# First expert tiles loaded in the blocks before, the last two blocks woven in another order, and the last tiles dealt otherwise among the dense experts

## The chip, the cores and the metric

The kernel runs on 1 core of one Trainium2 chip. The metric is device time in microseconds (us) of one execution, and the number compared is the median of several runs. A profile is one execution with the hardware profiler on. Its engines are PE (matrix multiply; PEld is its weight load), DVE (vector), ACT (scalar), POOL (GpSimd) and SP, which here only issues DMAs. "SPq" and "POOLq" in a profile are the queues of SP and POOL.

## The reference, cut to what matters

```python
h = tok_ref(x, W)              # 4 x 4096 tokens of width 256: patches, real FFT, one matmul
x1 = layernorm(h)
n  = layernorm(x1) * g + b
q, k, v = n @ Wq.T + bq, n @ Wk.T + bk, n @ Wv.T + bv
mem[t] = decay * mem[t-1] + k[t] * v[t]          # along 4096 tokens
x1 = x1 + q * mem
x1 = x1 + relu(layernorm(x1) @ W1.T + b1) @ W2.T + b2
h  = h + x1
t  = layernorm(h)
out = h + t
for e in range(8):             # each token uses 2 of 8 experts
    out += combine[:, e:e+1] * (gelu(t @ w1[e] + b1[e]) @ w2[e] + b2[e])
```

## The kernel before, in words

The 16384 tokens are 32 blocks of 512 (`Block`, numbers 0 to 31; `NB` = 32, `NS` = 31). A block goes through three stages, and three blocks are in work at once. In turn `i` of the main loop (L835) the newest block `new` = `i` is embedded (`embed`, L301 and L312), gets its q, k and v and the recurrence (`retention`, L341, matmuls L268), and is added to its residual (`residual`, transposes L391); block `mid` = `i - 1` goes through its MLP (`mlp_in`, L414, matmuls L268; `mlp_out`, L420, matmuls L426) and gives its tokens; block `old` = `i - 2` is routed: `rows` makes rows of 260 words, `logits` and `choose` pick two experts for each token, `place` (L539) finds each row's place and writes the rows to a buffer in device memory, `xbuf`, with eight indirect DMAs on POOL (L560).

Experts work on tiles of 256 rows of `xbuf` that belong to one expert. `take(n, ...)` (L606) makes a table on DVE of the tiles that are full by then and appends them to the list `tiles`: none with block 0's rows, one with block 1's, then four with each block's, and 18 with those of block 30, 131 in all. A tile (`Tile`) has four parts, and each has a counter in `at`:

- `load` (L666): three DMAs on SP. The expert's weights `w` (641.5 KB, L670, 5 buffers), the rows turned by a DMA transpose into `xh` (L677, 6 buffers), four words of each row into `xg` (L680). Addresses come from the table, so SP waits until DVE has written it; the first tile of a `take` also waits until that block's writes to `xbuf` have landed.
- `turn` (L683): ACT puts the halves of `xh` together as `xT` (L687, two copies).
- `enter` (L689): eight matmuls (L694; fp32, so the trace counts two for each) into a `p_mm` buffer, and two Gelu activations on ACT into `ge` (L702).
- `leave` (L706): eight matmuls (L711), then DVE adds the bias and multiplies by the token's share into `y` (L725, L727; 4 buffers), and POOL adds the rows to the output with two indirect DMAs (L731). These two wait until the last two such adds have landed, so tiles add one after the other.

`expert_step` (L807) with `n` tiles entered loads up to tile `n + 3` (`AHEAD` is 4), turns up to tile `n + 1`, enters tile `n` and leaves tile `n - 1`. In the loop it is called by `slot(known)`, four times a turn, once more than three tiles are pending and never so that it would turn a tile of this turn's own `take`. The first step is in turn 5, in its first slot.

SP, PE, DVE and ACT carry out their instructions in the order of the program text (`manual_schedule`); each is a queue in which a waiting instruction holds up all behind it. PSUM pools: `p_mm` has four buffers, for q, k, v, MLP input, `enter` and transposes; `p_tm` has three.

Turning a block from tokens to features is done in two ways. `split1` and `split2` (L330, L403) let ACT split it (L248), a DMA transpose on SP turn it (L256), and ACT or DVE join it (L262). `to_features` (L231) uses eight transposes on PE (L235) and two copies on ACT (L236).

After the loop (L888 to L918) block 31 is `last` and block 30 is `old`. In order: `features2` of 31; two steps; `features3`, `rows`, `logits`, `choose` of 30; a step; `mlp_in` of 31 with `place` and `take` of 30 after its first part (there also eight DMAs on SP that pad the ends of the experts' regions, L584) and a step after its fifth; `mlp_out` of 31 with a step between its halves. Then block 31's own experts: it is not routed through `xbuf`, each of the 8 experts is applied to all its 512 tokens (`Expert`, L743: `enter` 16 matmuls L761, `leave` 16 matmuls L778), and the eight `Expert` items are put into the list with two tiles between each two. Two more steps, `features3`, `logits`, `choose` and `combine` of 31 follow, then steps until the list is empty. The last `Expert` stores block 31 (L795), half on SP, half on ACT's queue.

Tiles are numbered below by their place in the list: 104 to 107 are entered in turn 31, 109 is the first tile with block 29's rows, 113 the first of the 18 with block 30's.

Of the kernel before, what the change touches and what calls it, by code (L numbers as in the profile page):

```python
# [30 lines left out]
def vit_tower_kernel(  # L31
# [20 lines left out]
    E = rw.shape[1]  # L52
    KD, KH = D // P, H // P
    J = STRIDE // 2
    TT = 4
# [10 lines left out]
    NB = B * NBLK  # L66
# [5 lines left out]
    NS = NB - 1  # L72
# [12 lines left out]
    def load_x(i):  # L85
        xb = xpool.tile([P, XW], F32, name="xb")
        nc.sync.dma_start(out=xb, in_=x[i // NBLK, i % NBLK])
        return xb
# [5 lines left out]
    with tc.tile_pool(name="prep", bufs=1) as prep:  # L94
# [8 lines left out]
        xs = {0: load_x(0)}  # L103
# [127 lines left out]
    def to_features(dst, src):  # L231
        for k in range(KD):
            ps = p_mm.tile([P, BLK], F32, name="mm")
            for t in range(TT):
                nc.tensor.transpose(ps[:, ts(t, P)], src[:, t, ts(k, P)], ident)  # L235
            nc.scalar.copy(dst[:, k, :], ps)  # L236
# [40 lines left out]
    class Block:  # L277
# [128 lines left out]

        def features2(self):
            self.hT = two.tile([P, KD, BLK], F32, name="hT")
            if self.i == 0:
                to_features(self.hT, self.zz)  # L410
                return
            self.turn.join(self.hT, nc.scalar.copy)
# [193 lines left out]
    def take(n, block, writes):  # L606

        k = FULL[n] - FULL[n - 1]
        if not k:
            return  # L610
        full = small.tile([1, E], F32, name="full")
        nc.vector.tensor_tensor(full, cnt[0:1, :], first[0:1, :E], ALU.subtract)
        if n == NS:
            nc.vector.tensor_scalar(full, full, float(S - 1), None, ALU.add)
        whole = small.tile([1, E], I32, name="whole")
        nc.vector.tensor_copy(whole, full)
        nc.vector.tensor_scalar(whole, whole, S.bit_length() - 1, None, ALU.arith_shift_right)
        nc.vector.tensor_copy(full, whole)  # L618

        nc.vector.tensor_tensor(full, full, taken, ALU.subtract)  # L620
        upto = small.tile([1, E + 1], F32, name="upto")
        nc.vector.memset(upto[:, 0:1], 0.0)
        nc.vector.tensor_tensor_scan(upto[:, 1:], ones_e, full, 0.0, ALU.mult, ALU.add)

        base = small.tile([1, E + 1], F32, name="base")
        nc.vector.tensor_tensor(base[:, :E], taken, upto[:, :E], ALU.subtract)
        nc.vector.tensor_scalar(base[:, E:], upto[:, E:], -1.0, None, ALU.mult)
        nc.vector.scalar_tensor_tensor(base, base, float(S), first[0:1, :], ALU.mult, ALU.add)
        step = small.tile([1, E], F32, name="step")
        nc.vector.tensor_tensor(step, base[:, 1:], base[:, :E], ALU.subtract)  # L630
        shape = [1, k, E]
        past = small.tile([1, KMAX, E], F32, name="past")[:, :k, :]
        nc.vector.tensor_tensor(
            past,
            tile_f[:, :k].unsqueeze(2).to_broadcast(shape),
            upto[:, 1:].unsqueeze(1).to_broadcast(shape),
            ALU.is_ge,
        )
        table_f = small.tile([1, 2, KMAX], F32, name="table_f")[:, :, :k]
        nc.vector.tensor_reduce(table_f[:, 0, :], past, AX.X, ALU.add)  # L640
        nc.vector.tensor_tensor(past, past, step.unsqueeze(1).to_broadcast(shape), ALU.mult)
        nc.vector.tensor_reduce(table_f[:, 1, :], past, AX.X, ALU.add)
        nc.vector.scalar_tensor_tensor(
            table_f[:, 1, :], tile_f[:, :k], float(S), table_f[:, 1, :], ALU.mult, ALU.add
        )
        table = four.tile([1, 2, KMAX], I32, name="table")[:, :, :k]
        nc.vector.tensor_scalar(table[:, 0, :], table_f[:, 0, :], float(P), float((E - 1) * P), ALU.mult, ALU.min)
        nc.vector.tensor_scalar(table[:, 1, :], table_f[:, 1, :], base[:, 0:1], None, ALU.add)
        if n < NS:
            nc.vector.tensor_scalar(upto, upto, float(k), None, ALU.min)  # L650
            nc.vector.tensor_tensor(taken, taken, upto[:, 1:], ALU.add)
            nc.vector.tensor_tensor(taken, taken, upto[:, :E], ALU.subtract)
        for t in range(k):
            tiles.append(Tile(table, t, block, writes if t == 0 else []))

    AHEAD = 4
    tiles = []
# [142 lines left out]
    at = dict(load=0, turn=0, enter=0, leave=0)  # L800

    def advance(what, upto):
        while at[what] < min(upto, len(tiles)):
            getattr(tiles[at[what]], what)()
            at[what] += 1

    def expert_step():  # L807

        n = at["enter"]
        advance("load", n + AHEAD)  # L810
        advance("turn", n + 2)
        advance("enter", n + 1)
        advance("leave", n)
# [3 lines left out]
    blocks = [Block(i) for i in range(NB)]  # L817
# [3 lines left out]
    def slot(known):  # L821

        if len(tiles) - at["enter"] > LEFT and at["enter"] + 2 <= known:
            expert_step()
# [7 lines left out]
    with tc.manual_schedule(engines=MANUAL):  # L832
        xs[1] = load_x(1)
        blocks[0].differences(xs.pop(0))
        for i in range(NB):  # L835
            new = blocks[i]
            known = len(tiles)
            mid = blocks[i - 1] if i >= 1 else None
            old = blocks[i - 2] if i >= 2 else None
            embed = new.embed()  # L840
            next(embed)
            if mid:
                mid.features2()
            if old:
                old.rows()
                old.turn3()
            next(embed)
            next(embed, None)
            slot(known)
            if old:  # L850
                old.join3()
            if i == 0:
                fold(wqkv_sb, G1, B1, BQ)
            for m in range(KH):
                if mid:
                    mid.mlp_in(m)
                if m == 1 and i:
                    new.split1()
                if m == TT - 1:
                    slot(known)  # L860
                if m == KH - 3:
                    new.features1()
            if old:
                for t in range(TT):
                    old.logits(t)
            if i + 1 < NB:
                blocks[i + 1].differences(xs.pop(i + 1))
            for m in range(KD):
                new.retention(m)
                if old and m == 0:  # L870
                    old.choose()
            if old:
                take(old.i + 1, old, old.place())
            if i + 2 < NB:
                xs[i + 2] = load_x(i + 2)
            slot(known)
            if mid:
                mid.mlp_out(0)
            new.residual()
            slot(known)  # L880
            if i == 0:
                fold(w1_sb.unsqueeze(1), G2, B2, MB1)
            else:
                new.split2()
            if mid:
                mid.mlp_out(1)

        last, old = blocks[NS], blocks[NS - 1]  # L888
        last.features2()
        expert_step()  # L890
        expert_step()
        old.features3()
        old.rows()
        for t in range(TT):
            old.logits(t)
        old.choose()
        expert_step()
        for m in range(KH):
            last.mlp_in(m)
            if m == 0:  # L900
                take(NS, old, old.place())
            if m == TT:
                expert_step()
        last.mlp_out(0)
        expert_step()
        last.mlp_out(1)

        for e in range(E):
            tiles.insert(len(tiles) - 2 * (E - 1 - e), Expert(e, last))
        expert_step()  # L910
        expert_step()
        last.features3()
        for t in range(TT):
            last.logits(t)
        last.choose()
        last.combine()
        while at["leave"] < len(tiles):
            expert_step()  # L918
# [82 lines left out]
```

## Time and profile before

| | |
|---|---|
| runs shown | 2304.29, 2302.86, 2296.04 us (median 2302.86) |
| the profiled execution | 2310.97 us |
| its span, from the first to the last instruction | 2309.2 us |
| PE matmul busy | 2196.0 us (95%) |
| PE weight load busy | 1573.8 us (68%) |
| DVE busy | 1468.9 us (64%) |
| POOL busy | 867.0 us (38%) |
| ACT busy | 790.2 us (34%) |
| DMA engines, busy share | 0.1 to 0.9, by slice |

Some 1.8 us of the execution lie outside its span. The execution that was profiled is 8.1 us above the median of the runs shown. In a group or timeline line the first number is the start (timeline) or the busy time (groups), then come engine, source line, operation, the tile written and the tiles read, sizes and a count; "[15.92 <-ACT xT L687]" behind a timeline line says that the engine had been idle for 15.92 us and that what ended the wait was ACT's instruction that wrote `xT`.

### The profile page before, as it was taken

The numbers are of one execution on the slowest core, as the hardware profiler recorded it, in microseconds if no ns is written. First come the engines' busy times: TensorE is split into PE (matmuls) and PEld (weight loads), VectorE is DVE, ScalarE is ACT, GpSimd is POOL, SyncE is SP. The second block draws the span as 40 slices with busy tenths as digits, with TensorE's granted clock in tenths as the row PEclk, the third lists the DMA queues.
The fourth block names the chain that finished last, engine by engine and source line by source line (L and its number), as shares of the span: only waits on it lengthen the run. The fifth ranks groups of instructions, "written<-read, shape, count | busy, mean of one in ns | idle before, by whom it ended". The sixth has DMA issues, their size and how long they took to land. (4 is left out here: it accounts for less than half of the span.)

```text
span 2309.2 us, 28330 instructions
## 1 busy us (share of the span) xinstructions
PE 2196.0 (95%) x8644; PEld 1573.8 (68%) x8644; DVE 1468.9 (64%) x4358; ACT 790.2 (34%) x1217; POOL 867.0 (38%) x828
## 2 busy tenths in 40 slices
PE   3999979999999999999999999999999999998994
PEld 3576647776676777767667777667677776766773
DVE  6566736666676667666666676666666766665442
ACT  0222233333344333333433333334433333343341
POOL 0012214444433444444344444443344444435334
PEclk8999989999999999999999999999999999999997
DMA  5133365566566765665666656656675566567895
GB/s 148 28 95 76 83 145 124 132 135 143 130 137 137 156 123 133 131 142 129 138 142 156 121 128 139 145 130 134 143 156 122 133 131 141 110 114 181 182 206 89
DMA packets 466920, 304.11 MB, mean 132 GB/s; under 512 B 380369, under 2 KB 434769, under 8 KB 462673
## 3 DMA queue, kind: packets, MB, share of 16 engines
q1 hardware_dynamic: 416864, 234.67, 42.6%
q0 software_dynamic: 49632, 67.39, 16.6%
q8 instruction: 68, 1.11, 0.2%
q14 instruction: 84, 0.68, 0.1%
q10 hardware_dynamic: 272, 0.26, 0.0%
HBM read 131.26 MB, written 88.39 MB: 95 GB/s over the span
## 5 line engine op out<-in xcount | busy, mean ns | idle before, releaser
L731 POOL DMA_INDIRECT out<-y,xg x262 | 435.1, 1661 | 558.0 <-DVE y L727 308.9
L426 PE MATMUL tm<-w_sb,aT 128*128 128x256 f32 x2048 | 462.5, 380 | 11.3 <-issue 7.9
L268 PE MATMUL mm<-hT,w_sb 128*128 128x512 f32 x1024 | 450.9, 593 | 1.7 <-ACT hT L262 1.4
L426 PEld LDWEIGHTS tm<-w_sb,aT 128*128 128x128 f32 x2048 | 386.9, 190 | 76.5 <-issue 23.0
L268 PEld LDWEIGHTS mm<-hT,w_sb 128*128 128x128 f32 x1024 | 194.6, 190 | 222.5 <-issue 211.6
L560 POOL DMA_INDIRECT xbuf<-row,to x248 | 242.7, 979 | 263.0 <-DVE full L618 189.5
L268 PE MATMUL mm<-hT,wqkv_sb 128*128 128x512 f32 x768 | 340.1, 599 | 1.3 <-DVE hT L262 1.2
L702 ACT ACTIVATE ge<-mm,w 128x256 f32<-128x256 f32 x262 | 109.6, 471 | 566.7 <-issue 565.8
L694 PE MATMUL mm<-xT,w 128*128 128x256 f32 x1048 | 256.6, 389 | 27.0 <-ACT xT L687 27.0
L268 PEld LDWEIGHTS mm<-hT,wqkv_sb 128*128 128x128 f32 x768 | 144.5, 191 | 172.2 <-issue 162.7
L418 ACT ACTIVATE aT<-mm,vec 128x512 f32<-128x512 f32 x256 | 172.3, 686 | 242.3 <-PE mm L268 237.5
L711 PE MATMUL tm<-w,ge 128*128 128x256 f32 x1048 | 248.0, 380 | 0.0
L694 PEld LDWEIGHTS mm<-xT,w 128*128 128x128 f32 x1048 | 198.4, 194 | 65.6 <-ACT xT L687 28.2
L312 PE MATMUL tm<-weff,xd 128*128 128x256 f32 x1024 | 229.8, 383 | 11.3 <-DVE xd L289 8.1
L312 PEld LDWEIGHTS tm<-weff,xd 128*128 128x128 f32 x1024 | 195.1, 192 | 42.3 <-DVE xd L289 8.5
L711 PEld LDWEIGHTS tm<-w,ge 128*128 128x128 f32 x1048 | 199.7, 191 | 30.9 <-issue 3.6
L687 ACT COPY xT<-xh 128x512 uint16<-128x512 uint16 x262 | 181.4, 762 | 42.2 <-DMA xh<-xbuf 42.2
L248 ACT COPY planes<-zz 128x1024 uint16<-128x1024 uint16 x124 | 123.5, 1043 | 155.3 <-DVE zz L222 155.1
L213 POOL TENSOR_SCALAR rstd<-mv 128x4 f32<-128x4 f32 x96 | 38.5, 401 | 333.7 <-DVE mv L207 331.5
L725 DVE TENSOR_TENSOR y<-tm,w 128x512 f32<-128x512 f32 x131 | 90.6, 691 | 99.6 <-PE tm L711 63.0
L301 PE MATMUL tm<-wsum,xb 128*128 128x256 f32 x512 | 120.4, 390 | 26.2 <-ACT wsum L118 26.2
L517 POOL TENSOR_TENSOR ex<-euler,second 128x4 f32<-128x4 f32 x32 | 34.5, 1080 | 270.3 <-DVE second L509 270.3
(139 smaller groups left out, 2273.1 us busy)
## 6 DMA issues: line engine op xcount, KB each, us to landing
w<-in_wex SPq DMA_DIRECT2D x139, 641.5 KB
xb<-in_x SPq DMA_DIRECT2D x32, 1040.0 KB
out<-h SPq DMA_DIRECT2D x31, 512.0 KB
out<-y,xg POOLq DMA_INDIRECT x262
xbuf<-row,to POOLq DMA_INDIRECT x248
xh<-xbuf SPq DMA_TRANSPOSE x131
xg<-xbuf SPq DMA_DIRECT2D x131, 4.0 KB
xbuf<-none SPq DMA_DIRECT2D x8, 260.0 KB
```

The costliest lines, as they stand in the source:

```text
L248: nc.scalar.copy(planes[:, :, i * D : (i + 1) * D], half)
L268: nc.tensor.matmul(ps, lhsT=w[:, k, ts(m, P)], rhs=rhs[:, k, :], start=k == 0, stop=k == KD - 1)
L301: nc.tensor.matmul(ps[:, u, :], lhsT=od[:, j, ts(u, P)], rhs=wsum[:, j, :], start=j == 0, stop=j == J - 1)
L312: nc.tensor.matmul(ps[:, i, :], lhsT=xd[:, i, j, ts(u, P)], rhs=weff[:, i * J + j, :], start=j == 0, stop=j == J - 1,)
L418: nc.scalar.activation(self.aT[:, m, :], ps, AF.Relu, bias=vec[:, MB1 + m : MB1 + m + 1])
L426: nc.tensor.matmul(ps[:, i, :], lhsT=self.aT[:, k, ts(u * 2 + i, P)], rhs=w2_sb[:, k, :], start=k == 0, stop=k == KH - 1,)
L560: write = nc.gpsimd.indirect_dma_start(out=xbuf, out_offset=bass.IndirectOffsetOnAxis(ap=to[:, c, t : t + 1], axis=0), in_=self.row[:, t, ...
L687: nc.scalar.copy(halves[:, :, :, 1 - i], self.xh[:, i * KD : (i + 1) * KD, :])
L694: nc.tensor.matmul(ps[:, m, :], lhsT=self.w[:, k * D + m * P : k * D + (m + 1) * P], rhs=self.xT[:, k, :], start=k == 0, stop=k == KD - 1,)
L702: nc.scalar.activation(self.ge[:, m, :], ps[:, m, :], AF.Gelu, bias=self.w[:, 5 * D + m : 5 * D + m + 1])
L711: nc.tensor.matmul(ps[:, c, :], lhsT=self.ge[:, k, ts(c, P)], rhs=w[:, (2 + k) * D : (3 + k) * D], start=k == 0, stop=k == KD - 1,)
L731: add = nc.gpsimd.indirect_dma_start(out=out, out_offset=bass.IndirectOffsetOnAxis(ap=self.xg[:, c, NUMBER - D : NUMBER - D + 1], axis=0), ...
```

## The change

Four edits. (1) In the loop, as long as no tile has been entered, up to two tiles are loaded ahead of `split2`. (2) The loop ends a turn earlier; turn 31 and the code after the loop are written as one piece in another order. Its steps are not held back by `slot`. (3) `features2` of block 31 uses `to_features`. (4) The tiles not yet loaded are dealt evenly ahead of the `Expert` items.

```diff
         def features2(self):
             self.hT = two.tile([P, KD, BLK], F32, name="hT")
-            if self.i == 0:
+            if self.i in (0, NS):
                 to_features(self.hT, self.zz)
                 return
...
-        for i in range(NB):
+        for i in range(NS):
...
             slot(known)
+            if at["enter"] == 0:
+
+                advance("load", 2)
             if i == 0:
                 fold(w1_sb.unsqueeze(1), G2, B2, MB1)
             else:
                 new.split2()
...
-        last, old = blocks[NS], blocks[NS - 1]
-        last.features2()
+        last, mid, old = blocks[NS], blocks[NS - 1], blocks[NS - 2]
+        embed = last.embed()
+        next(embed)
+        mid.features2()
+        old.rows()
+        old.turn3()
+        next(embed)
+        next(embed, None)
+        expert_step()
+        old.join3()
+        for m in range(KH):
+            mid.mlp_in(m)
+            if m == 1:
+                last.split1()
+            if m == TT - 1:
+                expert_step()
+            if m == KH - 3:
+                last.features1()
+        for t in range(TT):
+            old.logits(t)
+        expert_step()
+        mid.mlp_out(0)
+        old.choose()
+        expert_step()
+        mid.mlp_out(1)
+        take(NS - 1, old, old.place())
+        last.retention(0)
+        mid.features3()
+        mid.rows()
+        expert_step()
+        last.retention(1)
+        for t in range(TT):
+            mid.logits(t)
+        mid.choose()
+        last.residual()
         expert_step()
         expert_step()
-        old.features3()
-        old.rows()
-        for t in range(TT):
-            old.logits(t)
-        old.choose()
+        take(NS, mid, mid.place())
         expert_step()
+
+        last.features2()
         for m in range(KH):
             last.mlp_in(m)
-            if m == 0:
-                take(NS, old, old.place())
-            if m == TT:
+            if m in (1, 4):
                 expert_step()
+        expert_step()
         last.mlp_out(0)
         expert_step()
         last.mlp_out(1)

+        rest = tiles[at["load"] :]
+        del tiles[at["load"] :]
         for e in range(E):
-            tiles.insert(len(tiles) - 2 * (E - 1 - e), Expert(e, last))
+            tiles.extend(rest[len(rest) * e // E : len(rest) * (e + 1) // E])
+            tiles.append(Expert(e, last))
```

Counted through, the new piece has twelve steps up to the second half of `mlp_out` of 31 and two behind the dealing; they enter tiles 104 to 117. At the dealing tiles 0 to 118 are loaded, 12 are left, and they go ahead of the experts 0 to 7 as 1, 2, 1, 2, 1, 2, 1, 2. Expert 7 is the last item; tiles 129 and 130 stand ahead of it.

More of the change, by code (lines that the diff above doesn't have):

```diff
@@ L865, in vit_tower_kernel @@
                     old.logits(t)
-            if i + 1 < NB:
-                blocks[i + 1].differences(xs.pop(i + 1))
+            blocks[i + 1].differences(xs.pop(i + 1))
             for m in range(KD):
```

## The prediction

> **What bounds the kernel now.** I read the page first: PE is busy in every slice but a few. The windows then show the end, with the DMA engines' share and GB/s as the last two numbers: full, while PE works.
>
> ```profile
> PE   3999979999999999999999999999999999998994
> ```
>
> ```profile
> 2200.00:2210.00 10.00, 10.00 (x40) 7.30 (x39) 3.05 (x9) 5.59 (x10) 3.86 (x3) 1.00 0.99 222
> ```
>
> So time is won only where PE idles. The waits by length, then the timelines, give the places: one long stop of PE near 300 us, two short ones after 2090 us, and the end.
>
> ```profile
> 294.23 7.07 PE L312 MATMUL tm<-weff,xd 128*128 128x256 f32 x32
> 317.22 3.78 PE L694 MATMUL mm<-xT,w 128*128 128x256 f32 x8 [15.92 <-ACT xT L687]
> ...
> 2100.93 3.47 PE L694 MATMUL mm<-xT,w 128*128 128x256 f32 x8 [6.40 <-ACT xT L687]
> ...
> 2182.36 3.68 PE L694 MATMUL mm<-xT,w 128*128 128x256 f32 x8 [4.71 <-ACT xT L687]
> ...
> 2275.53 3.62 PE L778 MATMUL tm<-w,ret 128*128 128x256 f32 x16
> ```
>
> The reader is to see the three stops, that the eight matmuls behind each take 3.5 to 3.8 us in place of 1.89, and that PE ends at 2279.15, 30 us ahead of the span's end. Those 30 us are POOL's adds (L731), one tile after the other, as the chain of waits shows:
>
> ```profile
> 2281.21 4.25 DMA out<-y,xg
> ...
> 2288.14 3.86 DMA out<-y,xg
> ...
> 2299.28 1.54 POOL out L731
> ```
>
> The first adds of consecutive tiles start at 2174.50, 2184.10, ... 2299.28: 16 intervals, on average 7.8 us; the eight up to 2243.43 average 8.6 (full DMA engines), the last five 6.6.
>
> **First loads.** The first step's loads stand on SP behind four row transposes; ACT idles until they land.
>
> ```profile
> 299.59 2.63 ACT L262 COPY hT<-turned 128x512 uint16<-128x512 uint16 x4 [3.83 <-DMA turned<-planes]
> 302.09 1.98 ACT L453 COPY row<-tok 128x1024 uint16<-128x1024 uint16 x2
> 315.79 1.38 ACT L687 COPY xT<-xh 128x512 uint16<-128x512 uint16 x2 [11.72 <-DMA xh<-xbuf]
> ```
>
> With tile 0 loaded in turn 3 and tile 1 in turn 4, ACT's copy follows its row copies at 304.07 and not at 315.79: 11.7 us, all of it on PE, which had been idle from 301.3; 4.2 us of the stop stay. The three DMAs a tile now stand on SP ahead of `split2`'s transpose, which starts at 241.95 and 295.30. The writes that tile 0 waits for begin on POOL at 227.03, tile 1's at 280.38; the rows below put a tile's `xh` 11.6 us behind that and its three loads' end some 14.5: 241.5 and 294.9, just ahead. Nothing late follows; if each were a landing (4 us) late, `hT` at 299.59 would be too, and the gain 7.7. If the matmuls behind the shorter stop ran at full speed (behind 1.12 us at 283.77 they did), it were 14.3 (1.89 and 0.69 of slow matmuls less). I take 11.7, bounds 7.7 and 14.3.
>
> **Stops removed at the end.** The stop at 2100.93 is `hT` of block 31 (a transposing DMA that ACT awaits) ahead of the tile's copy: eight PE transposes (0.87 us, as the row of L235 between its neighbours) replace it, with two ACT copies of 0.53 for two of 1.0 and four of 0.66 and the transpose on SP. The one at 2182.36 is a late load: its buffer waited for DVE, DVE for `ex` on POOL behind adds. In the new order the same `ex` stands behind two tiles' adds too, but with one tile fewer behind it in DVE; I take both stops out. With the slow matmuls: 6.4 + 1.6 and 4.7 + 1.8.
>
> **Waits added: block 29's rows.** I lay the new order on the old clock, from 2057.23, where `logits` of block 29 end and the two orders part. A step is 3.46 us on PE (1.73 each for `enter` and `leave`), half of `mlp_out` 6.9, `retention` 5.15 a half, `logits` 1.71, transposes 0.87, a part of `mlp_in` 1.72, an expert 6.88. Two steps and both halves of `mlp_out` of 30 end on PE at 2077.95. Then DVE: sum and statistics 2.0, POOL's root 1.5, `tok` 1.4, `h` 1.25: `place` of 29 begins at 2084.2, where before it began at 2070.07, since it now stands behind block 30's tokens on DVE. Behind it go these rows:
>
> ```profile
> 2073.57 1.06 POOL L560 DMA_INDIRECT xbuf<-row,to  x1 [6.53 <-DVE full L618]
> ...
> 2121.67 1.00 POOL L560 DMA_INDIRECT xbuf<-row,to  x1 [0.30 <-issue]
> ```
>
> ```profile
> 2085.15 1.32 SPq L677 DMA_TRANSPOSE xh<-xbuf  x1
> ...
> 2136.10 1.27 SPq L677 DMA_TRANSPOSE xh<-xbuf  x1
> ```
>
> First write 3.5 after `place` begins, `xh` 11.6 after the first write, landing 4.3 (rows: 3.8 to 5.9): 2103.6. On SP the fifth step's three loads (nine DMAs) follow each other; behind them stands nothing that PE needs sooner. The fifth step, between the halves of `retention`, turns tile 109, so ACT waits there; behind it in ACT's queue are `ge` of 108 and `ks` of the second half. Copy 1.4, `ge` 0.7, `ks` 0.7, DVE's recurrence and product 3.1: PE's `residual` can begin at 2109.5. PE has 16.7 us of work from 2077.95 (`place` 0.36, 5.15, 0.87, a step, 5.15, 1.71): 14.9 us idle, the first 6.8 of them because `enter` of 108 needs the `p_mm` buffer of v, which DVE frees only behind `place` and `take`.
>
> **Waits added: block 30's rows.** DVE from 2109.5: `choose` 2.85, residual 3.75, root 1.5, `zz` 1.4, two sums 2.45, then `y` of 108: its adds start on POOL at 2123.2. Those of 109 wait for them (1.9 + 3.75 + 0.85), 2129.7; they take 3.7, and behind them POOL issues block 30's writes, from 2133.4. `xh` of 113 comes 11.6 after that (block 29) to 14.4 (2121.67 to 2136.10, with the padding): I take 13. Landing 4.0, copy and `ge` of 112 2.2: `enter` of 113 at 2152.6 (bounds 2151 to 2156.5). PE arrives there at 2135.2: from 2109.5, 0.87, two steps, 0.36, a step, 0.87, 1.2 for the copies of `hT`, two parts, a step, three parts. 17.4 us idle: the ninth step turns tile 113, 17 us of PE work behind `place`, where before 33 us lay between (2114.56 to 2147.74).
>
> The Trainium skill has a rate for such a load: "DMA: Bandwidth & Descriptors", sections "Latency and other measured facts" and "Anatomy of one DMA", give 261 GB/s for a transposing DMA and a fixed 2 us; for 262 KB that is 3.0 us by estimate. The rows above show 3.8 to 5.9. By the page the sum would be 2.3 us better.
>
> **The end.** From `enter` of 113 PE has 37 halves of a step (63.9), 5.15 + 13.8 + 2.6 for block 31, eight experts 55.0, and as before 2.8 for small gaps and slow matmuls, 1.8 for those behind the stop: 145.1. PE ends at 2297.7, less 11.7: 2286.0, 7 us later than before. Behind it: store issued 4.5 after PE's end (2279.15 to 2283.65), landing 3.75, as an unhurried add's, and 4.4 from the last landing (2304.8, when SP's wait ends) to 2309.2: 12.7, so 2298.7. The adds must also get there. Tile 115's start at 2188.6 (32.8 us of PE work behind 2152.6, 1.8 slow, 1.4 for DVE); then fifteen intervals. The dealing itself issues nothing more. There are now 2.375 weight loads in 11.6 us where there were 3 in 13.8, so less than the 8.6: I take 7.7 for eleven and 6.6 for the last four, 2299.7; with 10.0 to the end and 11.7 off, 2298.0. Both say 2298.7, against 2309.2: 10.5 us. On the median, 2302.86, that is 2292.4; the profiled time would be 2300.5.
>
> **Rivals.** (a) Block 30's wait is mostly covered, because writes and loads land sooner or PE arrives later: 17.4 + 1.8 less, 2273, and 2258 if block 29's is too. For it: ACT waited 8.74 us at 2140.10 before and PE none. Against: the 33 us that covered it are gone. (b) The adds set the end. Their fifteen intervals behind tile 115 must average under 8.15 to end no later than 2309.2; at the 9.2 of the slowest tiles before 2243 the last starts at 2326.6, 15.6 later than that, 2318. For it: the DMA share was 0.9 to 1.1 there. Against: fewer loads, and the last intervals are light. (c) The early loads hold up `split2`'s transposes, at `hT` a landing late (4.0), and `enter` of 113 is at its slow bound (3.9): 2300. For it: `hT` at 299.59 is itself awaited from SP's DMA, and the DMA share was 0.71 and 1.06 in the two 10-us windows from 2130, where 113's rows were written and read. Against: both would have to be at the slow end at once.
>
> **How the numbers follow.** Forecast 0.62, its own range 2284 to 2302 (the bounds of 113, of the loads, of 7.2 to 8.2 us an interval). (a) 0.18, (b) 0.10, (c) 0.10. A measurement of this kernel can tell 0.5% (11.5 us), and the forecast lies just inside: about half of it, 0.28, is faster, 0.34 the same. (a) is faster, (b) slower but for 0.02, (c) the same: 0.46 faster, 0.46 the same, 0.08 slower. The range, 2270 to 2308, leaves out most of (b) and the better part of (a).
>
> **What would show it.** Right: PE's stop at the first tile near 4 us; then a wait of L694 on the `p_mm` buffer near 7, one of L391 on `ret` near 8, one of L694 on `xT` near 17; PE's end 12 to 16 us ahead of the span's; intervals of adds near 7.7. Wrong: no stop of PE in front of tile 113, an `xh` of 109 or 113 issued before its block's last write, a first stop still above 10 us, or a stop of PE in the dense part, where I see none.

## The result and the profile after

| | before | after |
|---|---|---|
| median of the runs | 2302.99 us (4 runs, 2296.04 to 2304.29) | 2304.23 us (4 runs, 2300.57 to 2306.47) |
| the profiled execution | 2310.97 | 2304.22 |
| its span | 2309.2 | 2302.4 |
| start of the first tile's matmuls | 317.22 | 303.82 |
| from there to the end of block 29's `logits` | 1740.0 | 1733.3 |
| from there to the end of the span | 252.0 | 265.3 |

The ratio of after to before is 1.001, 95% interval 0.9986 to 1.0034: no difference that can be told. Forecast was 2292.4, with 2284 to 2302 as its own range and 2270 to 2308 as the range with the rivals; 2304.2 lies outside the first and inside the second. The three lower rows show that something did happen: the first tile starts 13.4 earlier, and the last three blocks take 13.3 longer. Below, "the common point" is the end of block 29's `logits` on PE, where the two orders part (2057.23 before, 2037.08 after).

First the timeline of PE of the changed kernel, at the places that the prediction named. The first two numbers are start and length, the bracket is the idle time in front of it.

```profile
303.82 3.78 PE L694 MATMUL mm<-xT,w 128*128 128x256 f32 x8 [4.11 <-ACT xT L687]
...
2089.70 1.76 PE L391 MATMUL tm<-ident,ret 128*128 128x128 f32 x7 [12.37 <-DVE lg L499]
...
2132.64 3.68 PE L694 MATMUL mm<-xT,w 128*128 128x256 f32 x8 [15.09 <-ACT ge L702]
...
2190.01 5.38 PE L778 MATMUL tm<-w,kv 128*128 128x256 f32 x16 [1.97 <-DVE y L725]
2198.47 3.78 PE L694 MATMUL mm<-xT,w 128*128 128x256 f32 x8 [3.08 <-ACT xT L687]
...
2282.47 3.62 PE L778 MATMUL tm<-w,ret 128*128 128x256 f32 x16
```

The stop of 15.92 at the first tile is down to 4.11. Of the two stops behind 2090 us, the one at block 31's `hT` is gone, but two others stand there, 12.37 at block 31's `residual` and 15.09 at tile 113, and the late load is still a stop, now in two parts behind 2188. The columns of the next view, the windows, are the window's length, then busy time and instructions of PE, PEld, DVE, ACT and POOL; the last three numbers are the granted clock, the DMA engines' share and GB/s.

```profile
2180.00:2190.00 10.00, 8.04 (x30) 5.25 (x29) 2.12 (x11) 3.12 (x5) 4.18 (x3) 1.00 0.41 43
2190.00:2200.00 10.00, 6.91 (x20) 5.38 (x21) 7.06 (x20) 2.07 (x4) 3.52 (x3) 0.71 1.03 256
2200.00:2210.00 10.00, 10.00 (x30) 6.93 (x29) 1.60 (x5) 3.48 (x6) 5.19 (x4) 0.78 0.82 193
```

The DMA engines are less than half busy for 10 us (0.41, 43 GB/s) while that load cannot be issued. In the two windows behind that the mean clock is 0.71 and 0.78, and the eight matmuls at 2198.47 take 3.78 where eight take 1.89 at the full clock: the stop cost more than its length. The chain of waits ends as before in POOL's adds:

```profile
2287.33 4.20 DMA out<-y,xg
...
2292.37 1.54 POOL out L731
```

Further back this view follows PE, because it puts the wait of tile 129's adds at 2285.38 down to DVE's `ms`, which is a dense expert's and which these adds don't need. Their own `y` was ready 6.5 us earlier (DVE, then POOL):

```profile
2278.24 0.62 DVE L727 TENSOR_SCALAR y<-y,tile_share 128x256 f32<-128x256 f32 x2
```

```profile
2285.38 1.65 POOL L731 DMA_INDIRECT out<-y,xg  x1 [3.10 <-DVE ms L786]
```

From tile 118 on every `y` was ready 6.5 to 13.3 us before its adds began, so in this stretch they waited for the adds ahead of them and not for PE.

Tile 115's adds start at 2171.62 and the last tile's at 2292.37: 15 intervals of 8.05 on average, where before the same 15 took 7.68 (2184.10 to 2299.28).

### The profile page after: what moved, and what is told of

Its sections match the earlier page's. It is cut to its first block, busy times and chain, and to the rows that moved or that the text cites. A ratio compares the mean times of both kernels' runs of the same rounds, so it can differ in the third digit from the quotient of the medians.

```text
span 2302.4 us, 28334 instructions
## 1 busy us (share of the span) xinstructions
PE 2195.0 (95%) x8652; PEld 1577.3 (69%) x8652; DVE 1464.1 (64%) x4358; ACT 785.3 (34%) x1213; POOL 864.2 (38%) x828
## 5 line engine op out<-in xcount | busy, mean ns | idle before, releaser
L426 PE MATMUL tm<-w_sb,aT 128*128 128x256 f32 x2048 | 453.1, 379 | 1.7 <-DVE h L433 1.7
L694 PE MATMUL mm<-xT,w 128*128 128x256 f32 x1048 | 257.5, 390 | 22.5 <-ACT ge L702 15.1
## 6 DMA issues: line engine op xcount, KB each, us to landing
w<-in_wex SPq DMA_DIRECT2D x139, 641.5 KB, 4.4
```

The costliest lines, as they stand in the source:

```text
L426: nc.tensor.matmul(ps[:, i, :], lhsT=self.aT[:, k, ts(u * 2 + i, P)], rhs=w2_sb[:, k, :], start=k == 0, stop=k == KH - 1,)
L694: nc.tensor.matmul(ps[:, m, :], lhsT=self.w[:, k * D + m * P : k * D + (m + 1) * P], rhs=self.xT[:, k, :], start=k == 0, stop=k == KD - 1,)
```

## Experiments

Two theories of what sets the end. A: PE does, with its stops. B: the chain of adds does; a stop of PE counts only as far as it makes that chain start later or slower. The twelve runs were made in three groups of four, with the kernel before beside each group; its medians there were 2312.03, 2309.14 and 2302.64, so times are compared as ratios. All times "after the common point" in the table are of one profiled execution each, and executions of one version differ: the profiled one of the early loads was the fastest of its six, 7.0 below their median, that of after lies at its median.

| run | ratio to before, 95% | PE ends | adds of tile 115 start | mean of 15 intervals | span ends |
|---|---|---|---|---|---|
| before | 1 | 221.9 | 126.9 | 7.68 | 252.0 |
| before again | | 224.1 | 128.8 | 7.16 | 246.1 |
| early loads only | 0.9947 (0.993 to 0.9964) | 222.7 | 128.2 | 7.06 | 244.2 |
| early loads, combine later | 0.9934 (0.9916 to 0.9953) | 219.4 | 127.4 | 7.59 | 251.2 |
| early loads, last adds left out | | 223.0 | | | 228.0 |
| after | 1.001 (0.9986 to 1.0034) | 249.0 | 134.5 | 8.05 | 265.3 |
| tail only | 1.005 (1.0033 to 1.0066) | 246.9 | 134.0 | 8.27 | 268.2 |
| after, combine later | 1.000 (0.9986 to 1.0014) | 240.9 | 134.9 | 7.81 | 262.1 |
| after, last adds left out | | 240.5 | | | 245.5 |
| after, last weights left out | | 239.1 | 133.1 | 7.01 | 249.1 |
| after, turn later | 0.9955 (0.994 to 0.997) | 239.3 | 126.1 | 7.86 | 254.1 |
| turn and combine later | 0.9966 (0.995 to 0.9982) | 231.4 | 125.4 | 7.92 | 254.0 |
| all three | 0.9997 (0.9983 to 1.0012) | 239.3 | 136.3 | 7.71 | 261.8 |
| all three, load ahead | 0.9948 (0.993 to 0.9966) | 228.4 | 124.5 | 8.03 | 254.9 |

**The kernel before, once more.** No edit.

> The kernel before, unchanged, profiled once more. If its first profiled execution (span 2309.2, 8 us over the median) was simply a slow one, the span is now 2300 to 2304 and the stretch from the first L694 matmul to the end of block 29's logits takes 1733 to 1735 instead of 1740.0. If the changed kernel is really quicker in that stretch, it takes 1740 again and the span stays at 2307 to 2310.

Neither expectation was met as a whole. The execution took 2307.14, span 2305.3; the stretch of the main loop took 1744.5, on a chip where three versions with the same loop (two of them with the early loads) took 1739.8 to 1742.3, and in the third group four versions took 1731.4 to 1732.9. So that stretch differs by 13 us between chips and executions, and the 6.7 that after seemed to win in it can't be put down to the change. The tail of this execution was 246.1, 5.9 shorter than in the first profile of before: its adds follow one another at 7.16, not 7.68.

**The parts of the change, one at a time.** Early loads alone are before with

```diff
             slot(known)
+            if at["enter"] == 0:
+                advance("load", 2)
```

> The kernel before plus the two early loads alone. If the early loads give what the prediction gave them: 10 to 13 less than before, 2290 to 2293. Rival (the late turns hold up other transposes, or the gain is lost behind the last adds): 2300 or more. First L694 matmul at 303 to 305 in both cases.

Measured 0.9947, which is 12.3 us of 2312.03. Its PE timeline at the first tile:

```profile
306.00 3.66 PE L694 MATMUL mm<-xT,w 128*128 128x256 f32 x8 [4.10 <-ACT xT L687]
```

The stop is 4.10, and the whole gain arrives at the end of the kernel (the expected 10 to 13 less; the absolute 2290 to 2293 was not met, since before itself took 2312.03 there). Next the opposite, after without these two lines:

```diff
-            if at["enter"] == 0:
-                advance("load", 2)
```

> The changed kernel without the two early loads, so the new order of the last three blocks and the dealing alone. If the early loads are worth 10 to 13 and the tail loses the same: 2314 to 2317, 11 to 14 over before. If the early loads are worth nothing at the end of the kernel: 2302 to 2305.

Measured 1.005, 11.6 us, as expected for a tail that loses what the early loads win. The two parts add up within their intervals (12.3 less, 11.6 more), so the small total is two large effects of opposite sign, and what has to be explained is the tail. The dealing of the dense items by itself was not tried: in the new order only 12 tiles are still to be loaded there, and the old way of inserting reaches further back.

**Does PE's stop at the late load matter?** In after the chain of this stop runs through POOL, then SP, then ACT; the three timelines:

```profile
2183.16 1.55 POOL L731 DMA_INDIRECT out<-y,xg  x1 [7.96 <-DMA out<-y,xg]
...
2186.00 1.63 POOL L517 TENSOR_TENSOR ex<-euler,second 128x4 f32<-128x4 f32 x1
```

```profile
2189.99 0.34 SPq L670 DMA_DIRECT2D w<-in_wex  x1
```

```profile
2197.04 1.38 ACT L687 COPY xT<-xh 128x512 uint16<-128x512 uint16 x2 [11.73 <-DMA xh<-xbuf]
```

`ex` of block 31 stands on POOL behind a tile's two adds, which waited 7.96 for the adds before them; `combine` on DVE needs `ex`, the `y` behind it on DVE frees the weight buffer, and only then SP can load. The edit puts two items between:

```diff
         last.choose()
+        expert_step()
+        expert_step()
         last.combine()
```

> The changed kernel with block 31's combine moved two dense items back, so that the loads of two more tiles are issued ahead of it on POOL's queue. Theory A (TensorE's stops set the end, the one at the first tile loaded behind combine among them): the stops at about 2190 to 2205 of some 9.9 go, and the time falls by 8 to 10 to 2294 to 2296. Theory B (the chain of accumulating stores sets the end): the last stores follow one another at 8 us all the same, and the time moves by -3 to +1, 2301 to 2305.

PE's timeline of this version at the same place:

```profile
2196.54 1.89 PE L694 MATMUL mm<-xT,w 128*128 128x256 f32 x8
2198.27 3.62 PE L778 MATMUL tm<-w,kv 128*128 128x256 f32 x16
```

No stop, full speed, and PE ends 8.1 earlier (240.9 for 249.0). But the span ends only 3.2 earlier and the time is 1.000 against 1.001, two intervals that overlap almost wholly. A asked for 8 to 10. The same edit on the early loads:

> The kernel before plus the early loads, with combine two items later. Theory A (the stop of TensorE at the tile loaded behind combine costs its 4 us in the end): 0.991 to 0.993 of the kernel before. Theory B (the chain of stores sets the end, which starts no earlier): as the early loads alone, 0.994 to 0.996.

0.9934, between the two ranges, and its interval reaches into both: it doesn't decide. PE ended 3.3 earlier than with the early loads alone; the span ended 7.0 later, but that of the early loads was the short execution named above.

**What would PE's path alone give?** The adds of the last 15 tiles are left out, in the new order and in the old with early loads:

```diff
+            if len(added) >= 2 * 116:
+                return
             before = added[-2:] + [self.block.stored]
```

> The changed kernel with the accumulating stores of tiles 116 to 130 left out (those rows lack their tiles' part); loads and products stay. If these stores set the end: the span ends 2 to 4 after the last store of h, 10 to 12 earlier counted from the end of block 29's logits (254 to 256 instead of 265.3). If besides they hold up the loads and so TensorE: its last matmul ends at least 3 earlier than 249.0 after that point; if not, within 1.5 of it.

> The kernel before plus the early loads, with the accumulating stores of tiles 116 to 130 left out (those rows lack their tiles' part). If the stores set the end in the old order too: the span ends 226 to 230 after block 29's logits instead of 244.2, 5 behind TensorE's last matmul. If TensorE's path set it: 240 or more.

The old order ends 228.0 after the common point, as expected, and the new one 245.5, some 9 earlier than expected, each 5.0 behind PE's last matmul. With the adds they ended at 244.2 and 265.3. So in both orders the adds put 16 to 20 on the end of the span (the 16 goes by the short execution of the early loads, so it is a lower end): B is right about what ends last. But PE's path itself is 17.5 longer in the new order, and the adds begin with it. (In the new order without these adds `ex` has nothing to wait for, so the stop at the late load is gone too: PE ends at 240.5, as with combine later. That is 8.5 earlier than in after, the second case of the expectation, and most of why the span came below its 254 to 256.)

**What makes the adds' intervals 8?** In after the weight loads of all tiles behind the 117th, and of the dense experts among them, are left out:

```diff
+            if len(loaded) <= 116:
                 wrow = nc.sync.value_load(...)
-                self.w = five.tile([P, NW], F32, name="w")
+                loaded.append(five.tile([P, NW], F32, name="w"))
...
+            self.w = loaded[-1]
```

> The changed kernel with the weight loads of all tiles behind the 117th and of the dense experts among them left out (they compute with the weights of the 117th tile, so their results differ); stores and other loads stay. If the stores' intervals are long because the weights' transfers share the DMA engines: those of the last ten fall from 7.8 to 6.3 to 6.8, and the span ends 8 to 16 earlier counted from block 29's logits (249 to 257 instead of 265.3). If the 8.05 is the stores' own: 7.6 to 8.1, and 262 to 265.

POOL's timeline of this version in the middle of the dense part (only the first of a tile's two adds; its source lines are moved by three or more), and a window there:

```profile
2197.28 1.54 POOL L734 DMA_INDIRECT out<-y,xg  x1 [3.43 <-DMA out<-y,xg]
...
2203.64 1.54 POOL L734 DMA_INDIRECT out<-y,xg  x1 [2.97 <-DVE h L798]
...
2210.00 1.58 POOL L734 DMA_INDIRECT out<-y,xg  x1 [2.97 <-DVE y L730]
...
2216.53 1.54 POOL L734 DMA_INDIRECT out<-y,xg  x1 [3.10 <-DVE tile_share L726]
```

```profile
2210.00:2245.00 35.00, 35.00 (x140) 26.32 (x139) 16.54 (x41) 12.74 (x23) 17.44 (x12) 1.00 0.38 46
```

Intervals of 6.4 and 6.5 with the DMA share at 0.38, while PE works as hard as ever (35.00 of 35). From 2236 on four of them were 7.1, 7.2, 8.3 and 8.6: the chain had caught up with PE, and three of these four waited for `y`; that is why the last ten came to 7.0 and not to 6.3 to 6.8. The span ended 249.1, 16.2 less than after; some 3 of that is the stop at the late load, which goes with the loads. In after itself the twelve intervals up to the last weight load averaged 8.40, the three behind it 6.65. The twelve hold one long one: tile 115's adds begin at 2171.62, tile 116's at 2183.16, 11.54 later, with two weight loads issued at 2171.00 and 2172.68; without these loads it is 7.39, and the other eleven average 8.12. So sharing the DMA engines with 641.5 KB loads stretches a tile's adds from 6.5 to some 8, and once to 11.5. The old order has the long interval too, but ahead of tile 115, between tiles 112 and 113, with two weight loads issued at 2155.00 and 2156.67 (POOL, before):

```profile
2155.61 1.67 POOL L731 DMA_INDIRECT out<-y,xg  x1 [4.32 <-DVE y L727]
...
2167.13 1.54 POOL L731 DMA_INDIRECT out<-y,xg  x1 [7.98 <-issue]
```

Of the 5.6 us that the fifteen intervals of after are longer than those of before, 3.8 are in the first. And shorter intervals would soon have met the other limit: without the last weights, where the adds had caught up with PE, the span still ended 10.0 behind PE's last matmul, against 16.3 in after.

**Are the two long stops needed?** ACT's timeline in after shows what stands behind the copies of tiles 109 and 113:

```profile
2083.68 1.38 ACT L687 COPY xT<-xh 128x512 uint16<-128x512 uint16 x2 [16.59 <-DMA xh<-xbuf]
2084.93 0.82 ACT L702 ACTIVATE ge<-mm,w 128x256 f32<-128x256 f32 x2
2085.64 0.69 ACT L356 ACTIVATE ks<-mm,vec 128x512 f32<-128x512 f32 x1
...
2130.51 1.38 ACT L687 COPY xT<-xh 128x512 uint16<-128x512 uint16 x2 [20.84 <-DMA xh<-xbuf]
2131.76 0.82 ACT L702 ACTIVATE ge<-mm,w 128x256 f32<-128x256 f32 x2
2132.48 1.84 ACT L418 ACTIVATE aT<-mm,vec 128x512 f32<-128x512 f32 x3
```

ACT waits 16.59 and 20.84 for rows just written, with work behind it (`ks` of block 31, its `aT`) that PE had made ready long ago. The edit lets these two steps turn only the tile that they enter:

```diff
-    def expert_step():
+    def expert_step(turned=2):
...
-        advance("turn", n + 2)
+        advance("turn", n + turned)
...
         mid.rows()
-        expert_step()
+        expert_step(1)
...
             if m in (1, 4):
-                expert_step()
+                expert_step(1 if m == 1 else 2)
```

> The changed kernel with ScalarE's copies of tiles 109 and 113 (the first tiles of block 29's and block 30's rows) moved behind the gelu of the tile ahead and behind the copies that block 31 needs. Theory B' (the ordered copies keep the gelu of tile 108 and block 31's work waiting for transfers, so the last stores start late): the wait of 12.4 on the residual goes, tile 113 starts 8 to 15 earlier, the time falls by 6 to 13 to 0.994 to 0.998 of the kernel before. Rival (the last stores are late for another reason, the row writes on POOL's queue among them): within 3 of the changed kernel, 1.000 to 1.002.

ACT and then PE in this version:

```profile
2072.18 0.85 ACT L702 ACTIVATE ge<-mm,w 128x256 f32<-128x256 f32 x2
2075.44 0.69 ACT L356 ACTIVATE ks<-mm,vec 128x512 f32<-128x512 f32 x1 [2.41 <-issue]
2089.73 1.38 ACT L687 COPY xT<-xh 128x512 uint16<-128x512 uint16 x2 [13.60 <-DMA xh<-xbuf]
```

```profile
2083.46 1.76 PE L391 MATMUL tm<-ident,ret 128*128 128x128 f32 x7 [2.78 <-DVE lg L499]
...
2128.52 3.78 PE L694 MATMUL mm<-xT,w 128*128 128x256 f32 x8 [7.92 <-ACT xT L687]
```

ACT waits as before, but now behind `ge` and `ks`. The residual's stop is down from 12.37 to 2.78 and tile 113's from 15.09 to 7.92. The residual comes 41.2 after the common point instead of 52.6, tile 113 86.2 instead of 95.6, the adds of tile 115 8.4 earlier, and the time falls from 1.001 to 0.9955, some 12.7 us. The place of these two copies in ACT's order is about the whole loss of the tail (11.6). With combine moved as well:

> The changed kernel with the copies of tiles 109 and 113 later and with combine two items later: TensorE's stop of 4.7 behind combine goes, its end comes 4 to 8 earlier than 239.3 after block 29's logits. Theory B (stores): the time as with the copies alone or 1 to 3 less, 0.994 to 0.9955. Theory A (TensorE): 4 to 8 less, 0.992 to 0.9935.

PE ends 7.9 earlier again (231.4 for 239.3), the span at 254.0 for 254.1, and the ratio is 0.9966: nothing gained. A falls here; B's range ends at 0.9955, and the interval of the ratio reaches into it.

**A version meant to be better.** Copies later, block 30 placed ahead of tiles 109 and 110, tiles 113 to 115 behind `mlp_in` of 31, combine later (the lines of `expert_step` and of combine are as above):

```diff
+        take(NS, mid, mid.place())
         expert_step()
         expert_step()
-        take(NS, mid, mid.place())
         expert_step()
...
         last.features2()
         for m in range(KH):
             last.mlp_in(m)
-            if m in (1, 4):
-                expert_step()
+            if m == 1:
+                expert_step(1)
         expert_step()
         last.mlp_out(0)
         expert_step()
+        expert_step()
```

> The changed kernel with the copies later, block 30's rows written as soon as they are chosen (ahead of tiles 109 and 110), tiles 113 to 115 behind block 31's first MLP products, and combine two items later. If what the new order costs is the waits for the two transfers of rows: 18 to 25 less than the changed kernel, 0.989 to 0.993 of the kernel before. Rival (the chain of stores bounds from tile 109 on, however early the rows are): no better than the early loads alone, 0.994 to 0.996.

It missed both ranges: 0.9997. SP and ACT, then PE, in this version:

```profile
2101.43 14.56 SPq L584 DMA_DIRECT2D xbuf<-none  x8
...
2117.99 1.27 SPq L677 DMA_TRANSPOSE xh<-xbuf  x1
```

```profile
2123.26 1.38 ACT L687 COPY xT<-xh 128x512 uint16<-128x512 uint16 x2 [19.06 <-DMA xh<-xbuf]
```

```profile
2125.86 5.69 PE L268 MATMUL mm<-hT,w_sb 128*128 128x512 f32 x8 [17.71 <-ACT hT L236]
```

I had overlooked that `place` of block 30 also puts eight filling writes on SP's queue (14.56 us), which now stood ahead of tile 112's loads: a new stop of 17.71, through ACT's order once more. One line ahead of `take` mends it:

```diff
+        advance("load", at["enter"] + AHEAD)
         take(NS, mid, mid.place())
```

> The last but one version (copies later, block 30's rows early, combine later) with tile 112's loads issued ahead of block 30's placing, whose eight filling writes stood on SP's queue in front of them. If that queue is what kept hT of block 31 waiting for 17.7: this stop goes and TensorE ends 220 to 226 after block 29's logits instead of 239.3. The time, if the chain of accumulating stores then sets the end as in the early loads' version: 0.992 to 0.996. If TensorE set the end: 0.989 to 0.992. If the stop stays: 0.999 to 1.001.

```profile
2101.83 5.40 PE L268 MATMUL mm<-hT,w_sb 128*128 128x512 f32 x8 [2.85 <-ACT hT L236]
```

In this PE timeline the stop is 2.85. PE ends 10.9 earlier than in the version without the line (228.4, a little later than the 220 to 226 expected), and the ratio is 0.9948, within the range given for B. No version of the tail beats the early loads alone (0.9947): the ratios from 0.9934 to 0.9966 all overlap, though PE's end among them differs by 20 us. The lowest, 0.9934, is before with early loads and combine later; it beats both kernels, but can't be told from the early loads alone.

## Why the prediction missed its size

The sum for the span was 2298.0: 305.5 for the first tile's start, 1740.0, and 252.5 behind the common point. Measured were 303.8, 1733.3 and 265.3. On the median, where the loop's luck of one execution falls away, the miss is 11.8 (2304.2 against 2292.4), about the tail's 12.8. The wait at block 31's `residual` and that at tile 113 were in the sum at nearly their size, so they are not in this miss, though moving the two copies takes back about as much (12.7).

- *First loads, 11.7.* Right: 0.9947 or 12.3, the stop 4.11 for 4.2. Rival (c), early loads that hold up other transposes, falls with the same run.
- *"I take both stops out."* Half right. The stop at `hT` went. The one at the late load stayed (5.05 in two parts for 4.71), since one tile fewer on DVE is no cure when the two adds ahead of `ex` on POOL wait 7.96 themselves. It was also named there as what would show the prediction wrong: a stop of PE in the dense part. It cost PE 8.1 (the version with combine later), which is nearly the whole error of PE's path, 153.5 for 145.1 from tile 113 to its end; in the one execution of each, 3.2 of that reached the end of the span.
- *Block 29's rows.* Right: the residual 52.6 after the common point for 52.3. The 6.8 at a `p_mm` buffer came as 0.78, in the second half of `retention`; the same idle time then stood in one piece at the residual.
- *Block 30's rows.* Right: tile 113 at 95.6 for 95.4, the stop 15.1 for 17.4. For its `xh` I took 4.0 to land; ACT's copy at 2130.51 stood 4.4 behind its issue at 2126.14, and the page of after has a median of 4.6 for this load. The 3.0 by estimate from the Trainium skill ("DMA: Bandwidth & Descriptors", sections "Latency and other measured facts" and "Anatomy of one DMA") is less than what is seen here; the second section gives its 2 us for DMAs issued from GpSimd, while these are issued from SP.
- *"I take 7.7 for eleven and 6.6 for the last four."* This is the term that failed: 111.1 expected, 120.75 measured, and tile 115's adds started 134.5 after the common point, not 131.4. Together 12.8, the miss. The twelve intervals beside weight loads were 8.40 on average, not 7.7: one of 11.54, which the sum had nothing for, and eleven of 8.12; that dealing leaves fewer loads per microsecond didn't make them shorter. Tile 115 was late because the sum gave DVE 1.4 behind PE's product where it took 4.2, 2.8 of the 3.1: `tok` and `h` of block 31 stood ahead of that `y` on DVE until 2169.98. The sum also lacked a second limit, which did not bind here since every `y` from tile 118 on was ready 6.5 us or more ahead: the 12 tiles left are dealt among 8 experts, so three tiles and two experts take 3 x 3.46 + 2 x 6.88 = 24.1 us, 8.05 a tile, where two tiles and an expert took 13.8 before, 6.9 a tile. The prediction's own "2.375 weight loads in 11.6 us" (it counted 11 tiles) means 8.4 a tile, and it didn't set that against its 7.7. Without the last weights the adds did meet this limit.
- *The base.* The tail of the first profile, 252.0, was itself 5.9 longer than the second; measured against 246.1, the new tail loses 19 in these two executions, and by the timed runs of the tail alone 11.6.
- *Rivals.* (b), the adds, was the right mechanism for the sum's error, and its threshold of 8.15 was missed by 0.1 only. (a), waits that are covered, didn't come true, yet the version with the copies later shows that part of it could have been had: ACT's wait stays, PE's are 2.78 and 7.92 for 12.37 and 15.09. Its price, 2273, was not reached: that version's ratio is 0.9955.

## What to carry to other kernels

Where a chain of stores trails the compute engine, price three things in the new order: when it starts, its interval beside the transfers that will be in flight then, and the pace at which work is handed to it; time saved on the compute engine alone (8.1 and 7.9 us here) may buy next to nothing. On engines that work in program order, a copy issued ahead for a transfer still on its way holds up everything behind it, so put it behind the work that others are waiting for; and when a step is moved, list every queue it issues on (here eight writes on SP). Profile the kernel before twice where the tail matters: two executions differed by 5.9 there.

## What the runs showed of the hardware

A tile's two accumulating indirect stores, each pair waiting for the pair ahead, need 6.2 to 7.2 us from one tile to the next, mostly near 6.5, when no weight load is in flight: 6.4 and 6.5 in the window above with PE at work (DMA share 0.38), 6.5, 6.5 and 7.0 at the end of after. Beside weight loads of 641.5 KB the intervals of one execution average 7.8 to 8.6 in the new order (seven executions, the one interval of 11 to 12 left aside). In the old order the first ten from tile 115 on average 8.22 and 7.43 (before, twice), 7.29 (early loads) and 8.14 (early loads, combine later). Why executions of nearly the same order differ by 0.9 is open; over ten such intervals it is about what their tails differ by (244.2 to 252.0).
